# Attention outputs with tokens on the partitions, the sums as a 17th column, and one transpose for the pieces of the maxima

## The chip, the cores and the metric

The kernel runs on one core of a Trainium2 chip. A core has five engines that work side by side, each through its own queue and in its queue's order: TensorE (PE; its weight loads are shown apart as PEld), VectorE (DVE), ScalarE (ACT), GpSimd (POOL) and SyncE (SP), which here only issues DMAs. Matrix products are written to PSUM, everything else lies in SBUF; both have 128 partitions. The metric is the device time of one execution in microseconds.

## The reference

A stack of four decoder layers over x of 16 batches, 128 tokens and 256 features, with a context of the same shape. Every attention has 16 heads of 16 features. Layer 0 attends over the features of one token, layer 1 twice with values rounded to 8 bits. The change is about the four plain attentions, two in layer 2 and two in layer 3:

```python
logits = jnp.einsum('bhqd,bhkd->bhqk', qh, kh) / jnp.sqrt(jnp.float32(depth))
if mask is not None:
    logits = logits + mask * -1000000000.0
attn = jax.nn.softmax(logits, axis=-1)
out = jnp.einsum('bhqk,bhkd->bhqd', attn, vh)
out = out.transpose(0, 2, 1, 3).reshape(Bq, Sq, D)
return out @ wo + bo
```

The first attention of layer 2 has one mask for all batches, the second a mask of keys by batch; of layer 3, the first has none and the second a mask of queries and keys under which a row may be empty. Each is followed by a residual sum, a normalization and, after the second of a layer, a feed-forward block.

## The kernel before

The 16 batches form 8 groups of two (GB = 2, NT = 256 tokens). A group's work is recorded as a list of steps, each with the engines that can do it, a price in microseconds for each, and the blocks that it reads and writes; `Plan.order` then lays out the steps of all groups once, before anything is issued, by those prices, by buffer space and by LEADS, a table of offsets by group and stage. Every engine gets its instructions in that fixed order, so the steps of several groups are interleaved, and a price that is off changes the order and not the work. Four PSUM buffers "pw" of 2 KB a partition and one "ps" of 8 KB serve all groups; "mq" are four small buffers for the pieces named below; everything else lies in one arena in units of 512 B a partition.

TensorE takes fp32 operands here. A matmul uses the whole 128x128 array, or 32 rows of it (four row strips side by side, in the scores), or 32 columns (four column strips, in the products with the values).

A plain attention (`plain_attention`) makes qT and keys with features first: qT is [128 features, 2, 256 tokens], and kz keeps for each pair of heads two copies of the keys, each with the other head's rows zero, so that a strip of 32 rows holds a pair and one of its heads is picked by the copy. The values vz have tokens first; in the attentions over the context, keys and values are made early (`kept_context`), stored to DRAM and loaded again. Then, for each batch j (`batch`):

1. First scores (L833): queries by keys, for all 16 heads, into "ps". VectorE takes the negated maximum of every query and head (L1236; with the common mask in two halves at L1246 and L1251).
2. The 16 maxima of a query are split into three bf16 pieces whose sum is the fp32 number (`split`, L1261 to L1264, POOL or VectorE), written into "mq" as 4 x 128 columns, where head f of strip s has its three pieces at columns 32 s to 32 s + 2 of its own 128. Four bf16 transposes (L1271) turn them and ACT or DVE copies them out as mt (L1275).
3. Second scores, keys by queries: masks where there are any, then the matrix `three`, which adds up three rows of each strip, times mt, 512 columns wide and four strips side by side (L844), then kz by qT on top (L833), all into "ps" again. So the maxima are subtracted inside the matmul, and ACT's exp (L1302, or L1299 after a mask) gives eT with keys on the partitions.
4. Products (`products`, L879): the step `both` multiplies eT by the values and by `ones2`. The values, 32 columns with one of a pair of heads each and zeros for the other, are the stationary operand, 128 columns of eT move, four column strips side by side: 16 matmuls give the outputs with features first and 16 more the sums, already spread over the 16 features of each head.
5. VectorE takes the reciprocal of the sums, 128x256 (L1314), and multiplies (L1315) into oT, which is features first, as the output projection (`tokens_first`, L688) wants it.

The groups' other matmuls are `features_first` (L675), `tokens_first` (L688) and `transposed` (L647, four fp32 transposes of 128x128 and a copy by ACT or DVE at L654).

Of the kernel before, what the change touches and what calls it, by code (L numbers as in the profile page):

```python
# [66 lines left out]
SLOTS = {"sm": (64, 46), "row": (128, 12), "pw": (2048, 4), "ps": (8192, 1), "mq": (1024, 4)}  # L67
# [8 lines left out]
    [83, 27, 167, 130, 306, 193, 74, 226, 213, -45, 163, -53, 159, -84, 116, -64, 214, 400, 286, 283],  # L76
    [-69, -856, -114, -260, -60, 57, -165, -14, -2, -22, -386, -90, 144, -71, -260, -59, -586, -159, -213, -106],
    [49, -47, -11, 314, -162, 407, 51, 168, -361, -27, -172, 141, -4, -107, 36, 5, -54, 235, 78, 92],
    [-16, -228, 250, -173, -19, 106, 36, 203, -176, 14, 164, 2, 299, -144, 10, 309, -45, 154, 150, -1],
    [210, 166, 422, 222, 201, 790, 324, 499, 569, 334, 435, 116, 502, 205, 259, 760, 536, 716, 652, 178],  # L80
    [330, 158, 210, 147, 392, 517, 262, 488, 490, 57, 292, 77, 380, 208, 348, 38, 542, 447, 523, 1141],
    [267, 148, 130, 158, 333, 376, 220, 605, 204, -29, 43, 216, 340, 164, 196, 435, 324, 999, 754, 951],
    [288, 156, 593, 320, 407, 313, 255, 389, 233, 323, -30, 86, 440, 164, 213, 583, 372, 760, 452, 550],
# [344 lines left out]
def decoder_stack_kernel(ctx: ExitStack, tc: tile.TileContext, a: dict, out: bass.AP):  # L428
# [20 lines left out]

    ones2 = const.tile([P, 2, 32], F32, tag="ones2", name="ones2")  # L450
    G.memset(ones2, 0.0)
    for i in range(2):
        G.memset(ones2[:, i, DH * i : DH * i + DH], 1.0)
# [42 lines left out]
    three = const.tile([P, P], BF16, tag="three", name="three")  # L496
    mod = const.tile([P, 32], F32, tag="mod", name="mod")
# [10 lines left out]
    kept = {n: [[drams.tile([P, 4 * NT], F32, tag=f"{n}{g}{i}", name=f"{n}{g}{i}") for i in range(2)] for g in range(NG)] for n in ("mha2", "ca")}  # L508
# [17 lines left out]
    def prepare():  # L526
# [22 lines left out]
        def masks():  # L549

            G.tensor_scalar(later[:, 0:1], mod[:, 0:1], -1.0, 1.0, ALU.mult, ALU.add)
            G.tensor_tensor(later[:, 1:2], later[:, 0:1], mod[:, 1:2], ALU.subtract)
            G.tensor_tensor(three, mod[:, 0:1].to_broadcast([P, P]), mod[:, 1:2].to_broadcast([P, P]), ALU.add)
            G.tensor_tensor(three, three, mod[:, 2:3].to_broadcast([P, P]), ALU.add)

            G.tensor_scalar(m1, m1, -1.0e9, 1.0, ALU.mult, ALU.mult)

        step([("POOL", 2.5, masks)], reads=[raw, dl_token], writes=[mask_token], least=110.0)


# [306 lines left out]
    def products(eTs, vz, j, po, ones=False):  # L867

        def issue():
            for c in range(2):
                for i in range(2):
                    for s in range(4):
                        if ones:
                            lhsT = ones2[:, i, :]
                        else:
                            lhsT = vz.ap()[:, j, 4 * c + s, 2 * i : 2 * i + 2, :].rearrange("p a d -> p (a d)")
                        T.matmul(  # L879
                            po.ap()[32 * s : 32 * s + 32, 2 * ones + c, :], lhsT=lhsT,  # L880
                            rhs=eTs[c].ap()[:, 2 * s + i, :], start=(i == 0), stop=(i == 1),
                        )

        return issue

# [261 lines left out]
    def keys_and_values(kvT, wk, wv, biases, kz, vz):  # L1147
        pk, pv = psum(), psum()
        features_first(weight(wk), kvT, pk, reads=[bias_token], holds=[kz])
        for c in range(2):  # L1150

            def act(c=c):
                for par in range(2):
                    A.activation(
                        kz.ap()[:, c, par, :], pk.ap()[:, c, :], AF.Identity,
                        bias=biases[:, 2 + 2 * par + c : 3 + 2 * par + c], scale=parity[:, par : par + 1],
                    )

            def dve(c=c):
                for par in range(2):  # L1160
                    V.tensor_scalar(
                        kz.ap()[:, c, par, :], pk.ap()[:, c, :], parity[:, par : par + 1],
                        biases[:, 2 + 2 * par + c : 3 + 2 * par + c], ALU.mult, ALU.add,
                    )

            step([("ACT", 0.95, act), ("DVE", 1.06, dve)], reads=[pk], writes=[(kz, c)])
        tokens_first(weight(wv), kvT, pv, holds=[vz])

        def put(eng):
            for j in range(GB):  # L1170
                dst, src = place(vz, j, pv.ap()[:, j, :], None)
                eng(dst, src)

        step([("ACT", 0.8, lambda: put(A.copy)), ("DVE", 0.84, lambda: put(V.tensor_copy))], reads=[pv], writes=[(vz, "v")])

    def kept_context(g, cT):

        there = {}
        for n, layer, at, att in (("mha2", 2, 4, 1), ("ca", 3, 0, 2)):
            plan.enter(after=[*cT.writer.values()], w=RING - 1, kz=1, vz=1)  # L1180
            plan.stage -= 1
            for s in plan.steps[-1:]:
                s.stage = CONTEXT
            plan.special = CONTEXT
            kz, vz = block("m", [P, 2, 2, NT], role="kz"), values(F32)
            wk, wv = (a[w] for w in SQUARE[layer][at + 1 : at + 3])
            keys_and_values(cT, wk, wv, bias_qk[ATT[att]], kz, vz)
            there[n] = []
            for t, d, shape in ((kz, kept[n][g][0], "p c i k -> p (c i k)"), (vz, kept[n][g][1], "p j n q d -> p (j n q d)")):
                token = plan.token()  # L1190
                there[n].append((d, token))
                step([("SP", 2.0, lambda t=t, d=d, shape=shape: nc.sync.dma_start(out=d[:, :], in_=t.ap().rearrange(shape)))], reads=[t], writes=[token])
            plan.special = None
        return there


    def plain_attention(x, qxT, kvT, ws, biases, mask=None, masked=None, cost=0.9, masked_T=None, key_mask=None, held=(), may_be_empty=False, there=None):
# [5 lines left out]
        vz = values(F32) if there is None else block("m", [P, GB, 8, 4, DH], role="vz")  # L1203
# [9 lines left out]
        else:  # L1213
            for t, (d, token) in zip((kz, vz), there):
                step(
                    [("SP", 2.0, lambda t=t, d=d: nc.sync.dma_start(
                        out=t.ap().rearrange("p c i k -> p (c i k)" if len(t.shape) == 4 else "p j n q d -> p (j n q d)"), in_=d[:, :]))],
                    reads=[token], writes=[t] if t is kz else [(t, "v"), (t, "zero")],
# [3 lines left out]
            after=[*qT.writer.values(), *kz.writer.values()], w=1, oT=1, eT=SPREAD, r=1, mt=1, **({"e": 1} if mask is not None else {})  # L1222
        )
        wo = weight(wo)
        oT = block("m", [P, 2, NT], role="oT")

        def batch(j):
# [4 lines left out]
            m, rest, mq = small(16), small(16), block("mq", [P, 4, P], BF16)  # L1232
# [25 lines left out]
            def split(eng, m=m, rest=rest, mq=mq):  # L1258
                piece = lambda n: mq.ap().rearrange("p f (s r) -> p s f r", r=32)[:, :, :, n]
# [7 lines left out]
            pt, mt = block("pw", [P, 4, S], BF16), block("m", [P, 4, S], BF16, role="mt")  # L1267

            def turn(pt=pt, mq=mq):
                for f in range(4):  # L1270
                    T.transpose(pt.ap()[:, f, :], mq.ap()[:, f, :], ident_b)  # L1271

            step([("PE", 0.25, turn)], reads=[mq], writes=[pt], holds=[mt])
            step(
                [("ACT", 0.6, lambda pt=pt, mt=mt: A.copy(mt.ap(), pt.ap())), ("DVE", 0.62, lambda pt=pt, mt=mt: V.tensor_copy(mt.ap(), pt.ap()))],  # L1275
                reads=[pt], writes=[mt],
            )


            def below(ps, mt=mt):  # L1280
                if masked_T is not None:
                    laid(ps, *masked_T)
                laid(ps, lambda s: three[strip(s), :], lambda s: mt.ap()[strip(s)], start=masked_T is None)

            eTs = [block("m", [P, 8, S], role="eT") for _ in range(2)]
            pT, issue = scores(below, lambda r, c, i: kz.ap()[r, c, i, tok], lambda r, c: qT.ap()[r, c, tok], False)
            step(
                [("PE", 1.1 if masked_T is None else 2.1, issue, "rows")],
# [17 lines left out]
            po = block("pw", [P, 4, S])  # L1306
            r = block("m", [P, 2, S], role="r")

            def both(eTs=eTs, po=po, j=j):
                products(eTs, vz, j, po)()  # L1310
                products(eTs, vz, j, po, ones=True)()

            step([("PE", 1.76, both, "cols")], reads=[*eTs, (vz, "v"), (vz, "zero")], writes=[po], holds=[r])
            step([("DVE", 1.75, lambda po=po, r=r: V.reciprocal(r.ap(), po.ap()[:, 2:4, :]))], reads=[po], writes=[r])  # L1314
            step([("DVE", 0.42, lambda po=po, r=r, tok=tok: V.tensor_tensor(oT.ap()[:, :, tok], po.ap()[:, 0:2, :], r.ap(), ALU.mult))], reads=[po, r], writes=[(oT, j)])  # L1315

        for j in range(GB):
            batch(j)
        ps = psum()
# [150 lines left out]
```

## Time and profile before

| | |
|---|---|
| time, median of 3 runs | 1461.99 us (1459.98 to 1463.36) |
| the profiled execution | 1458.82 us, its span 1456.7 us |
| PE busy | 1398.3 us, 96% of the span |
| DVE, ACT, POOL busy | 1010.9, 849.7, 633.3 us |
| mean granted TensorE clock | 0.993 |
| products of plain attention, PE (L879, fp32) | 4096 matmul records in 64 steps |
| reciprocal of the sums, DVE (L1314) | 64 of 1752 ns |
| product with the reciprocal, DVE (L1315) | 64 of 421 ns |
| transposes of the pieces, PE (L1271) | 256 records in 64 steps |
| copies of them, ACT (L1275) | 64 of 582 ns |

Records of matmuls overlap, because they are pipelined: the time that a step takes from PE is read from the start of its first matmul to the start of the next step's. An fp32 matmul leaves two records, a bf16 one and a transpose leave one. The granted clock is the share of full speed that the chip let TensorE run at. In a line of a timeline the columns are the start, the time to the end of the last, engine, line, operation, output and input, shapes and the number of records.

### The profile page before, as it was taken

To read this page: it belongs to the slowest core of one execution; us is meant where nothing else is said; L and a number is where in the kernel's file an instruction comes from. 1 tells how busy PE (TensorE), PEld (TensorE's weight loads), DVE (VectorE), ACT (ScalarE), POOL (GpSimd) and SP (SyncE) were. 2 spreads that over 40 slices of the span, in tenths; PEclk is the share of its full clock that TensorE was granted. 3 is DMA by queue.
4 is the path that set the end of the run, shared out by engine and by line. 5 is a ranking of instruction groups with operands and counts; after the bars stand their busy time and mean duration, and the time that the engine had idled before them with its cause. 6 is when DMAs were issued, how large, how long until landed. Compare 5 with 4: busy or idle time off the path is not lost. (4 is left out here: it accounts for less than half of the span.)

```text
span 1456.7 us, 35756 instructions
## 1 busy us (share of the span) xinstructions
PE 1398.3 (96%) x14771; PEld 1141.3 (78%) x14771; DVE 1010.9 (69%) x1555; ACT 849.7 (58%) x1490; POOL 633.3 (43%) x1415
## 2 busy tenths in 40 slices
PE   8899998999899999899999999999999999999998
PEld 6677887878678888687878777777878888787777
DVE  1665788898988779767764976779478766556431
ACT  4565676766776656565554665657556454445552
POOL 2232857455777446524432542545634234243210
PEclk9999998999999999999999999999999999999999
DMA  6566513412432122112211532211210111100000
GB/s 207 138 171 192 188 48 102 117 34 67 125 90 95 44 67 70 56 52 66 84 38 45 160 101 97 85 55 56 73 45 2 42 38 66 31 31 2 2 9 23
DMA packets 138386, 109.67 MB, mean 75 GB/s; under 512 B 72288, under 2 KB 127472, under 8 KB 138096
## 3 DMA queue, kind: packets, MB, share of 16 engines
q1 hardware_dynamic: 138224, 107.40, 24.5%
q8 instruction: 116, 1.90, 0.5%
q14 instruction: 46, 0.38, 0.1%
HBM read 80.11 MB, written 27.26 MB: 74 GB/s over the span
## 5 line engine op out<-in xcount | busy, mean ns | idle before, releaser
L688 PE MATMUL pw<-arena 128*128 128x256 f32 x2048 | 484.2, 387 | 7.3 <-ACT arena L654 3.1
L675 PE MATMUL pw<-arena 128*128 128x256 f32 x2048 | 480.9, 385 | 7.8 <-ACT arena L663 2.5
L688 PEld LDWEIGHTS pw<-arena 128*128 128x128 f32 x2048 | 383.0, 192 | 68.8 <-issue 9.3
L675 PEld LDWEIGHTS pw<-arena 128*128 128x128 f32 x2048 | 379.2, 191 | 71.0 <-issue 10.0
L1133 POOL TENSOR_SCALAR arena<-arena,sm 128x128 f32<-128x128 f32 x512 | 195.9, 403 | 107.7 <-DVE sm L1127 73.4
L1314 DVE RECIPROCAL arena<-pw 128x256 f32<-128x256 f32 x64 | 112.1, 1752 | 104.0 <-PE pw L879 86.8
L734 POOL TENSOR_TENSOR arena<-arena,rows 128x512 f32<-128x512 f32 x107 | 137.7, 1289 | 89.7 <-ACT arena L721 74.0
L833 PE MATMUL ps<-arena 32*128 32x128 f32 (+2 forms) x3328 | 153.0, 309 | 2.8 <-DVE arena L1112 1.1
L1236 DVE TENSOR_REDUCE sm<-ps 128x16 f32<-128x2048 f32 x48 | 109.6, 2283 | 36.3 <-PE ps L833 33.8
L833 PEld LDWEIGHTS ps<-arena 32*128 32x128 f32 x3072 | 116.1, 186 | 20.4 <-issue 12.0
L696 DVE TENSOR_TENSOR arena<-pw,arena 128x512 f32<-128x512 f32 x88 | 60.3, 685 | 101.2 <-PE pw L688 99.7
L801 ACT ACTIVATE arena<-pw,cols_sb 128x256 f32<-128x256 f32 x184 | 78.0, 472 | 68.3 <-PE pw L675 65.5
L1261 POOL CAST mq<-sm 128x16 bf16<-128x16 f32 x58 | 15.8, 273 | 234.2 <-DVE sm L1236 114.6
L710 POOL TENSOR_SCALAR sm<-sm 128x2 f32<-128x2 f32 x88 | 20.6, 234 | 215.0 <-DVE sm L705 200.1
L721 ACT ACTIVATE arena<-arena,sm,sm 128x256 f32<-128x256 f32 x149 | 83.2, 597 | 49.3 <-POOL sm L714 48.7
L663 ACT ACTIVATE arena<-pw,cols_sb 128x256 f32<-128x256 f32 x140 | 72.7, 563 | 50.5 <-PE pw L647 47.0
L1275 ACT COPY arena<-pw 128x512 bf16<-128x512 bf16 x64 | 37.3, 582 | 84.5 <-PE pw L1271 77.6
L879 PE MATMUL pw<-arena 128*32 128x128 f32 (+1 forms) x2560 | 82.9, 265 | 3.4 <-ACT arena L910 3.0
L1099 DVE TENSOR_REDUCE sm<-ps 128x8 f32<-128x1024 f32 x64 | 77.6, 1213 | 9.8 <-PE ps L833 9.5
L1302 ACT ACTIVATE arena<-ps 128x1024 f32<-128x1024 f32 x64 | 64.1, 1025 | 33.1 <-PE ps L833 30.3
L647 PE MATMUL pw<-ident,arena 128*128 128x128 f32 x416 | 66.8, 286 | 15.1 <-DMA arena<-in_x_dram 5.1
L910 ACT COPY arena<-pw 128x1024 bf16<-128x1024 bf16 x56 | 56.3, 1011 | 41.9 <-PE pw L905 37.2
(142 smaller groups left out, 1993.8 us busy)
## 6 DMA issues: line engine op xcount, KB each, us to landing
arena<-in_L_xattn_ff_w_dram SPq DMA_DIRECT2D x38, 256.0 KB, 3.0
mha<-arena SPq DMA_DIRECT2D x16, 512.0 KB, 4.5
ca<-arena SPq DMA_DIRECT2D x16, 512.0 KB, 3.9
arena<-mha SPq DMA_DIRECT2D x16, 512.0 KB, 4.4
arena<-ca SPq DMA_DIRECT2D x16, 512.0 KB, 4.5
dqkv<-arena SPq DMA_DIRECT2D x8, 768.0 KB, 4.0
arena<-dqkv SPq DMA_DIRECT2D x16, 384.0 KB, 4.3
arena<-in_L_xattn_W_dram SPq DMA_DIRECT2D x24, 256.0 KB, 2.8
```

The source lines that it names most:

```text
L663: ("ACT", 0.54, lambda c=c: A.activation(dst.ap()[:, c, :], ps.ap()[:, c, :], AF.Identity, bias=biases(c), scale=scales(c))),
L675: T.matmul(ps.ap()[:, m, :], lhsT=w.ap()[:, k, m * P : (m + 1) * P], rhs=t.ap()[:, k, :], start=(k == 0), stop=(k == 1),)
L688: T.matmul(ps.ap()[:, j, :], lhsT=lhs(k, j) if lhs else t.ap()[:, k, j * S : (j + 1) * S], rhs=w.ap()[:, k, :], start=start and j + k == 0 ...
L721: ("ACT", 0.6, lambda j=j: A.activation(xh.ap()[:, j, :], x.ap()[:, j, :], AF.Identity, bias=nb.ap()[:, j : j + 1], scale=rstd.ap()[:, j : ...
L734: ("POOL", 1.33, lambda: G.tensor_tensor(dst.ap(), src.ap(), row(name), op)),
L801: "ACT", 0.47, lambda ps=ps, h=h, m=m, bias=bias: A.activation(h.ap()[:, m, :], ps.ap()[:, m, :], func, bias=bias),
L833: T.matmul(ps.ap()[:, s, c] if i is None else ps.ap()[:, s, c, i], lhsT=left(r, c) if i is None else left(r, c, i), rhs=right(r, c), start ...
L879: T.matmul(po.ap()[32 * s : 32 * s + 32, 2 * ones + c, :], lhsT=lhsT, rhs=eTs[c].ap()[:, 2 * s + i, :], start=(i == 0), stop=(i == 1),)
L1099: step([("DVE", 1.22, lambda: V.tensor_reduce(paired(m.ap()), ps.ap()[:, :, c], AX.X, ALU.max, negate=True))], reads=[ps], writes=[m])
L1133: G.tensor_scalar(e.ap()[:, q, :], e.ap()[:, q, :], r.ap()[:, q : q + 1], MAGIC, ALU.mult, ALU.add)
L1236: V.tensor_reduce(m.ap(), ps.ap().rearrange("p s c i k -> p (s c i) k"), AX.X, ALU.max, negate=True)
L1314: step([("DVE", 1.75, lambda po=po, r=r: V.reciprocal(r.ap(), po.ap()[:, 2:4, :]))], reads=[po], writes=[r])
```

## The change

The change concerns step 2 to 5 of every plain attention.

- Values are stored as [tokens, batch, head, 17]: 16 features and a column of ones (`values_with_one`). The kept values shrink from 1024 to 544 numbers a partition. The zeros between the heads and `ones2` go.
- Products: for each head one whole-array matmul, with eT (keys by queries, 128x128) stationary and the head's 17 columns moving. The result po has queries on the partitions: [128, 16 heads, 17], the 17th being the sum.
- VectorE takes the reciprocal of the 16 sums of a query and multiplies 128x256 outputs by it, in one step, into `on`, tokens first. After both batches `transposed` turns `on` into oT with four fp32 transposes and a copy.
- The pieces of the maxima of all 16 heads are packed in 128 columns, strip s having 12 at 32 s. One transpose turns them. In the second scores, `three_of[:, f]` (four matrices, made once on POOL) adds up the three rows of head f of each strip: 16 matmuls of 128 columns, in four rounds of four strips, between the ones of the keys, in the place of 4 of 512 columns.
- The prices of steps are changed where the step is; that of the products stays 1.76. LEADS is another table.

```diff
-SLOTS = {..., "mq": (1024, 4)}
+SLOTS = {..., "mq": (256, 4)}
...
+            for f in range(4):
+                t = three_of[:, f, :]
+                G.tensor_tensor(t, mod[:, 3 * f : 3 * f + 1].to_broadcast([P, P]), mod[:, 3 * f + 1 : 3 * f + 2].to_broadcast([P, P]), ALU.add)
+                G.tensor_tensor(t, t, mod[:, 3 * f + 2 : 3 * f + 3].to_broadcast([P, P]), ALU.add)
...
+    def values_with_one(made):
+        vz = block("m", [P, GB, H, DH + 1], role="vz")
+        if made:
+            step([("POOL", 0.3, lambda: G.memset(vz.ap()[:, :, :, DH : DH + 1], 1.0))], writes=[(vz, "one")])
+        return vz
...
-            pt, mt = block("pw", [P, 4, S], BF16), block("m", [P, 4, S], BF16, role="mt")
-                for f in range(4):
-                    T.transpose(pt.ap()[:, f, :], mq.ap()[:, f, :], ident_b)
+            pt, mt = block("pw", [P, S], BF16), block("m", [P, S], BF16, role="mt")
+            step([("PE", 0.1, lambda pt=pt, mq=mq: T.transpose(pt.ap(), mq.ap(), ident_b))], reads=[mq], writes=[pt], holds=[mt])
...
-                laid(ps, lambda s: three[strip(s), :], lambda s: mt.ap()[strip(s)], start=masked_T is None)
+                for f in range(4):
+                    c, i = divmod(f, 2)
+                    for part in (0, 1) if i else (1, 0):
+                        for s in range(4):
+                            r = strip(s)
+                            T.matmul(
+                                pT.ap()[:, s, c, i], lhsT=kz.ap()[r, c, i, tok] if part else three_of[r, f, :],
+                                rhs=qT.ap()[r, c, tok] if part else mt.ap()[r],
+                                start=..., stop=...,
+                            )
...
-            po = block("pw", [P, 4, S])
-            r = block("m", [P, 2, S], role="r")
+            po, r = block("pw", [P, H, DH + 1]), small(16)
             def both(eTs=eTs, po=po, j=j):
-                products(eTs, vz, j, po)()
-                products(eTs, vz, j, po, ones=True)()
+                for n in range(H):
+                    T.matmul(po.ap()[:, n, :], lhsT=eTs[n // 8].ap()[:, n % 8, :], rhs=vz.ap()[:, j, n, :], start=True, stop=True)
-            step([("PE", 1.76, both, "cols")], ...)
-            step([("DVE", 1.75, lambda po=po, r=r: V.reciprocal(r.ap(), po.ap()[:, 2:4, :]))], reads=[po], writes=[r])
-            step([("DVE", 0.42, ... V.tensor_tensor(oT.ap()[:, :, tok], po.ap()[:, 0:2, :], r.ap(), ALU.mult))], ...)
+            step([("PE", 1.76, both)], reads=[*eTs, vz], writes=[po], holds=[on])
+            def shares(po=po, r=r, j=j):
+                V.reciprocal(r.ap(), po.ap()[:, :, DH])
+                V.tensor_tensor(
+                    on.ap()[:, j, :].rearrange("p (h d) -> p h d", d=DH), po.ap()[:, :, 0:DH], r.ap().unsqueeze(2).to_broadcast([P, H, DH]), ALU.mult,
+                )
+            step([("DVE", 0.65, shares)], reads=[po], writes=[r, (on, j)])
         for j in range(GB):
             batch(j)
+        transposed(on, lambda t: t, copied, oT)
         ps = psum()
         tokens_first(wo, oT, ps)
```

## The prediction

> **What bounds the kernel now.** I read the busy shares of the page first. TensorE's queue is busy 96% of the span and VectorE 69%; in the chain of waits nearly every late step is PE work at L675 and L688 with no wait ahead of it.
>
> ```profile
> PE 1398.3 (96%) x14771; PEld 1141.3 (78%) x14771; DVE 1010.9 (69%) x1555; ACT 849.7 (58%) x1490; POOL 633.3 (43%) x1415
> ...
> L1314 DVE RECIPROCAL arena<-pw 128x256 f32<-128x256 f32 x64 | 112.1, 1752 | 104.0 <-PE pw L879 86.8 <-ACT arena L1302 14.6 <-issue 1.3
> ```
>
> So PE's time is counted at full price and VectorE's at next to nothing: the reciprocal that shrinks stood idle 104 us waiting, mostly for PE. PE's records overlap, so I take a step's price from start to start in the timeline of PE late in the run, where eight groups are interleaved and PE hardly waits.
>
> ```profile
> 1404.65 0.38 PE L688 MATMUL pw<-arena 128*128 128x256 f32 x1
> 1404.96 1.08 PE L879 MATMUL pw<-arena 128*32 128x128 f32 x32
> 1405.85 1.06 PE L879 MATMUL pw<-arena,ones 128*32 128x128 f32 x32
> 1406.84 1.04 PE L844 MATMUL ps<-m3T,ident_b 128*128 128x512 bf16 x4
> 1407.81 0.39 PE L844 MATMUL ps<-arena,three 32*128 32x512 bf16 x4
> 1408.04 1.06 PE L833 MATMUL ps<-arena 32*128 32x128 f32 x32
> 1409.03 0.40 PE L1271 MATMUL pw<-ident_b,mq 128*128 128x128 bf16 x4
> 1409.26 0.43 PE L688 MATMUL pw<-arena 128*128 128x256 f32 x1
> ```
>
> See three things. An fp32 matmul leaves two records (16 matmuls, x32), each with its own weight load; I call one a pass. Values and ones together take 1.88 us (1404.96 to 1406.84). And the pass before them holds PE for 0.31 us where such passes else follow each other every 0.216 us (next fence: 56 in 12.10 us): changing from the whole array to strips costs 0.095 us, and about 0.11 us of the 1.88 is the same on the way back, so the products themselves are 1.77 us.
>
> ```profile
> 1440.72 12.10 PE pw L688 x56
> ```
>
> What matters for the new form is how long a whole-array fp32 weight load takes when no long matmul hides it. First the groups by form (mean ns of one after the comma), then the loads and the matmul of one step that starts after a wait:
>
> ```profile
> L688 PEld LDWEIGHTS pw<-arena 128*128 128x128 f32 x2048 | 383.0, 192 | 68.8 <-issue 9.3 <-ACT arena L654 3.9 <-ACT arena L1105 2.1
> ...
> L879 PEld LDWEIGHTS pw<-arena,ones 128*32 128x32 f32 x2048 | 57.2, 110 | 0.0
> ```
> ```profile
> 79.24 0.48 PE L688 MATMUL pw<-arena 128*128 128x256 f32 x1 [0.28 <-DVE arena L696]
> ```
> ```profile
> 79.24 0.30 PEld L688 LDWEIGHTS pw<-arena 128*128 128x128 f32 x2 [0.49 <-DVE arena L696]
> ```
>
> A 128-column load is recorded 82 ns longer than a 32-column one: 0.85 ns a column, 109 ns for 128. At 79.24 the first matmul is 0.48 us where its group's mean is 0.387, and two loads span 0.30 us where one is 0.19: the second starts 0.108 us after the first. In the middle of a run 216 ns of streaming hide those 108 ns.
>
> Last, the granted clock, which, once the start is over, falls to a half four times before the last matmul, in stretches of 3.41 us or a multiple. The first line of each pair is the stretch before, the second the half-clock one; the last pair shows a thin stretch that was not followed by a drop.
>
> ```profile
> 50.46:53.88 3.42, 0.55 (x5) 1.00 0.90 264
> 53.88:57.29 3.41, 3.41 (x36) 0.50 0.21 55
> ...
> 589.77:593.18 3.41, 1.76 (x14) 1.00 0.62 231
> 593.18:596.60 3.42, 3.42 (x20) 0.50 0.00 0
> 842.36:845.77 3.41, 1.55 (x11) 1.00 0.00 0
> 845.77:849.18 3.41, 3.41 (x124) 1.00 0.14 14
> ```
>
> The stretch at 589.77 holds 4 fp32 transposes, 2 mask matmuls of 512 columns and 8 bf16 transposes, which stream 4 x 107 + 2 x 213 + 8 x 53 ns = 1.28 us, 0.38 of it; the one at 842.36 streams 1.39 us, 0.41. So a stretch in which the array streams under about 0.39 of the time cost the next one half its clock, though PE was far from idle in it.
>
> **The change, part by part.**
>
> *Products.* 64 times (8 groups, 4 attentions, 2 batches) 32 strip matmuls become 16 whole-array ones with 17 columns moving: 32 passes. A pass streams 216 x 17/256 = 14 ns and waits for its own load, 108 ns: 3.46 us for 1.77, +1.69 each, +108 us in all. Lower bound: passes as short as a strip's load, 0.85 x 32 = 27 ns, 0.87 us, -58 us; upper: loads not overlapped at all, their whole record of 192 ns, 6.1 us, +277 us. I take 108 ns: it is the same operation, only with a short stream behind it. The step's price in the kernel's plan stays 1.76 us, so the order written from it has PE early; nothing waits longer for that but PE's own successors.
>
> [...]
>
> *Shape changes.* The two orders of instructions have 495 changes of array shape before and 410 after: 85 x 0.095 = -8 us.
>
> *Transposes of the outputs.* 32 attentions gain four fp32 transposes; four such at L647 go from start to start in 0.50 us:
>
> ```profile
> 1416.83 0.66 PE L647 MATMUL pw<-ident,arena 128*128 128x128 f32 x4
> 1417.33 1.89 PE L688 MATMUL pw<-arena 128*128 128x256 f32 x8
> ```
>
> +16 us. They wait for VectorE's shares of the second batch, and output projection and residual wait for them; behind them in PE's queue stand other groups' matmuls. The wait is new, but po is now normalized in one short step instead of 1752 + 421 ns, so it starts 1.5 us sooner.
>
> *Maxima.* Four bf16 transposes (1409.03 to 1409.26, 0.23 us) become one: -0.17 x 64 = -11 us.
>
> *Second scores.* 1407.81 to 1409.03 is 1.22 us for the sums of pieces and the keys. After: 8 rounds of four strips for the keys at 0.11 (the 0.99 us of L833 over 8, less the 0.1 on the way out), 4 bf16 rounds of 128 columns at 0.056, and twice a key load that a short bf16 round covers only half, 0.05: 1.22. Zero, with -0.2 (bf16 rounds wholly hidden) to +0.3 us (every change of type exposes a load) as ends: -13 to +19 us.
>
> *Costed at nothing.* VectorE loses about 1.5 us x 64 = 96 us (reciprocal and division, 2.17, for 16 reciprocals and a 128x256 product, about 0.65), all beside PE. ScalarE's copy of the pieces halves (64 x 0.3 saved), 32 copies of 0.59 us come; at 58% it has room. POOL gets eight more mask operations of 0.4 us (the row of L553), 3.2 us once, some 200 us ahead of the first scores at 315, and smaller memsets (L861 takes 0.52 now). On SP the kept values go from 512 to 272 KB a transfer. Were that cover gone, the mask operations would cost 3 us and the copies 19.
>
> *Stalls.* PE's waits that the groups show sum to some 50 us, 32 of them after 320 us where attention runs (380, 400 and 357 us that hold 367, 389 and 348 us of busy PE). A PE that is slower by 100 us while VectorE has 96 us less to do waits less: -12 us, between 0 and -30.
>
> Sum: 108 - 8 + 16 - 11 + 0 - 12 = +93. The profiled execution took 1458.8 us (span 1456.7), the median shown is 3.2 above it: 1552 profiled, 1555 as a median, if the clock stays.
>
> *The clock.* It need not stay. In a product step the array streams 14 of 108 ns, 0.13. A step is 3.46 us, a stretch 3.41. With neighbours that stream 0.93 (the rest being stalls and shape changes, 50 + 47 us of 1457), a stretch falls under 0.39 when products fill more than (0.93 - 0.39) / (0.93 - 0.13) = 0.68 of it. With stretches that start anywhere, that happens in 2 x 0.32 = 0.65 of the steps: 42 stretches at half clock, each losing up to 1.7 us, less where the stretch holds the rest of a product step; at 1.55, +65 us, 1620. If loads count as activity too, it is 0 and the time 1555. Rows say "streaming": the 14 matmuls at 589.77 had their loads as well, and PE's queue was busy 1.76 of 3.41 us.
>
> [...]
>
> **Rivals.**
> - *The clock holds* (1555): for it, nothing before runs load-bound, so no row shows whether loads count. Chance 0.33.
> - *Loads overlap better than I think* and a pass takes 55 ns, as the plan's price implies (1.76 / 32). Then the step costs what it did, the sum is -8 + 16 - 11 - 12 = -15 and the time about 1447; it ends faster from 62 ns a pass down (64 x 32 passes: 2.05 us of time for each ns). Against it: 108 ns at 79.24. Chance 0.05.
> - *Low stretches chain*: half clock stretches the next product step, which keeps the clock down. Twice as many half stretches would give 1685. Chance 0.06; the stretch after is mostly full work, which let the clock back at once at 57.29 and 596.60.
>
> **How the numbers follow.** Likeliest, 0.56: products at 108 ns and about 42 half-clock stretches, 1620, its own range 1590 to 1650. The range given reaches down to the case of the steady clock with its second scores at the low end (1555 - 15) and up to 1655. A difference under 0.2% is about what a measurement of this kernel can't tell from no change; only the second rival ends faster, and between it and 1540 there is little: faster 0.04, same 0.01, slower 0.95.
>
> **What would show it.** Load records of the products at 190 ns starting every 108 ns and steps of about 3.4 us; PEclk digits under 9 through the slices from 320 us on, and a mean granted clock near 0.95 (42 x 3.41 us at half). Wrong if product passes start faster than 60 ns, or if the clock stays at 0.99.

## The result and the profile after

The changed kernel takes 1682.8 us, median of 4 runs; the kernel before, on the same chip, 1462.7. The ratio is 1.150 (95% interval 1.148 to 1.152); it leaves out one of the four runs, which took 1707.9 us at a granted clock of 0.910, where the others had 0.924 to 0.926. The profiled execution took 1681.8 us, its span 1680.0, against 1458.8 and 1456.7.

First the busy shares of the page of after, and the row of the granted clock over 40 slices of the span.

```profile
PE 1614.3 (96%) x13427; PEld 1359.3 (81%) x13427; DVE 921.5 (55%) x1564; ACT 835.4 (50%) x1460; POOL 615.8 (37%) x1422
...
PEclk9999979799989999799998989899989888999989
```

TensorE has 1344 matmul records fewer and is busy 216 us longer, at the same 96% of the span; VectorE has 89 us less to do. The clock falls under 9 in 12 of 40 slices, in the kernel before in one; its mean went from 0.993 to 0.924. Then the groups by form (busy us, mean ns of one, idle time ahead and what ended it).

```profile
L1319 PEld LDWEIGHTS pw<-arena 128*128 128x128 f32 x2048 | 252.5, 202 | 6.6 <-issue 2.4 <-DVE arena L790 0.3 <-ACT arena L802 0.3
L1319 PE MATMUL pw<-arena 128*128 128x17 f32 x2048 | 250.7, 270 | 0.0
...
L1324 DVE RECIPROCAL sm<-pw 128x16 f32<-128x16 f32 x64 | 16.5, 257 | 255.7 <-PE pw L1319 255.7
```

The reciprocal became seven times shorter, 257 ns for 1752, and the time that VectorE stands idle in front of it grew from 104 to 256 us, all of it waiting for the products. Two product steps from PE's timeline, the first at full clock, the second at half:

```profile
834.03 0.81 PE L689 MATMUL pw<-arena 128*128 128x256 f32 x3
834.68 3.64 PE L1319 MATMUL pw<-arena 128*128 128x17 f32 x32
838.17 0.59 PE L845 MATMUL ps<-m3T,ident_b 128*128 128x512 bf16 x2
```
```profile
677.72 1.06 PE L676 MATMUL pw<-arena 128*128 128x256 f32 x2
678.57 6.85 PE L1319 MATMUL pw<-arena 128*128 128x17 f32 x32
685.35 0.61 PE L845 MATMUL ps<-arena,three 32*128 32x512 bf16 x4
```

From 834.68 to 838.17 is 3.49 us for 32 passes, one every 109 ns; from 678.57 to 685.35 it is 6.78, about 212 ns a pass. The step was 1.77 us before.

**Where the 223 us of span came from.** For every kernel below I added up the starts of PE's matmul records by step, each from its first record to the next step's. The work at full clock is, for each kind of step, the lower quartile of its steps outside the half-clock stretches, times their number. What a step took over that inside a half-clock stretch is loss to the clock, up to half of its time; what is left is waits. By this rule:

| us of span | work at full clock | loss to the clock | waits |
|---|---|---|---|
| before, 1457 | 1329 | 10 | 96 |
| after, 1680 | 1453 | 121 | 83 |
| difference | +124 | +111 | -13 |

(The span's beginning and end, some 22 us, lie outside.) The clock's column is firm to some 4 us. Work and waits trade some 10 to 20 us when the same traces are grouped into steps another way (by line, output and number of records, before comes to 1341, 10 and 84, after to 1458, 124 and 75), so smaller differences between these two columns say little. About half of the loss is work, nearly all of it in the products, and half is the clock. The granted clock itself says the same: (1 - 0.924) x 1680 = 128 us against (1 - 0.993) x 1457 = 10. The list of waits shows nothing of either: PE's largest single line in it is 5.7 us.

**How the clock falls.** Five stretches of 3.41 us of after (length, PE's busy time and records, granted clock, share of the DMA engines, GB/s):

```profile
672.96:676.37 3.41, 3.41 (x29) 1.00 0.25 76
676.37:679.79 3.42, 3.42 (x13) 0.50 0.00 1
679.79:683.20 3.41, 3.41 (x18) 0.50 0.00 0
683.20:686.61 3.41, 3.41 (x24) 0.50 0.00 0
686.61:690.03 3.42, 3.42 (x31) 0.50 0.00 0
```

And three others, the first of which lies all but wholly inside one product step:

```profile
744.55:747.96 3.41, 3.41 (x33) 1.00 0.00 0
747.96:751.37 3.41, 3.41 (x19) 0.51 0.00 0
751.37:754.79 3.42, 3.42 (x17) 0.99 0.00 0
```

By its records PE is busy for all 3.41 us of each. But the share of the time in which the array streams at least one matmul's columns (an estimate: 0.833 ns a column for an fp32 pass at full clock, half of what passes of 256 columns take at half clock, where they follow each other every 427 ns at L676, and every 216 at full; half of that in bf16, of which 512 columns take 426 and 216 ns at L845) is 0.26 at 672.96, 0.71 at 676.37, 0.13 and 0.45 in the two after it, and 0.94 at 686.61, behind which the clock is full again. The stretch inside the product step streams 0.13, the next is half-clocked, streams 0.83, and the clock is let back.

### The profile page after: what moved, and what is told of

Same layout as the page of the kernel before. It is cut to its first block, busy times and chain, and to the rows that moved or that the text cites. A ratio compares the mean times of both kernels' runs of the same rounds, so it can differ in the third digit from the quotient of the medians.

```text
span 1680.0 us, 32904 instructions
## 1 busy us (share of the span) xinstructions
PE 1614.3 (96%) x13427; PEld 1359.3 (81%) x13427; DVE 921.5 (55%) x1564; ACT 835.4 (50%) x1460; POOL 615.8 (37%) x1422
## 4 chain that ended last, share of the span: by engine, by line
PE 88%; DVE 5%; ACT 2%; POOL 2%; issue 1%; DMA 1%; SPq 0%; POOLq 0%; DVEq 0%; ACTq 0%
PE pw L676 26%; PE pw L689 26%; PE pw L1319 14%; PE ps L1290 6%; PE ps L834 5%; PE pw L648 4%; PE ps L845 2%; PE pw L910 2%; POOL arena L1138 1%; DVE sm L1104 1%; DVE arena L1117 1%; PE pw L1024 1%; PE pw L991 1%; ACT arena L967 1%; DVE arena L966 1%
## 5 line engine op out<-in xcount | busy, mean ns | idle before, releaser
L676 PE MATMUL pw<-arena 128*128 128x256 f32 x2048 | 502.1, 398 | 5.5 <-ACT arena L915 1.8
L689 PE MATMUL pw<-arena 128*128 128x256 f32 x2048 | 495.8, 395 | 6.9 <-DVE arena L1003 3.6
L676 PEld LDWEIGHTS pw<-arena 128*128 128x128 f32 x2048 | 395.7, 199 | 70.0 <-issue 4.1
L689 PEld LDWEIGHTS pw<-arena 128*128 128x128 f32 x2048 | 394.2, 198 | 70.1 <-issue 5.8
L1319 PEld LDWEIGHTS pw<-arena 128*128 128x128 f32 x2048 | 252.5, 202 | 6.6 <-issue 2.4
L1319 PE MATMUL pw<-arena 128*128 128x17 f32 x2048 | 250.7, 270 | 0.0
L1324 DVE RECIPROCAL sm<-pw 128x16 f32<-128x16 f32 x64 | 16.5, 257 | 255.7 <-PE pw L1319 255.7
L1290 PE MATMUL ps<-arena 32*128 32x128 f32 x2048 | 110.7, 327 | 7.2 <-ACT arena L1311 5.7
L655 ACT COPY arena<-pw 128x512 f32<-128x512 f32 x75 | 43.5, 585 | 143.9 <-PE pw L648 139.1
L802 ACT ACTIVATE arena<-pw,cols_sb 128x256 f32<-128x256 f32 x190 | 80.6, 472 | 63.2 <-PE pw L676 60.1
L1290 PEld LDWEIGHTS ps<-arena 32*128 32x128 f32 x2048 | 85.4, 210 | 26.4 <-issue 12.9
L648 PE MATMUL pw<-ident,arena 128*128 128x128 f32 x544 | 94.2, 308 | 8.9 <-POOL bias_qk L579 5.1
L1311 ACT ACTIVATE arena<-ps 128x1024 f32<-128x1024 f32 x64 | 64.1, 1024 | 74.6 <-PE ps L1290 64.0
L834 PE MATMUL ps<-arena 32*128 32x256 f32 (+1 forms) x1280 | 93.9, 404 | 5.8 <-DVE arena L1117 5.5
```

Source lines behind the costliest of these rows:

```text
L648: T.transpose(p[:, c, j * S : (j + 1) * S], s[:, j, c * P : (c + 1) * P], ident)
L676: T.matmul(ps.ap()[:, m, :], lhsT=w.ap()[:, k, m * P : (m + 1) * P], rhs=t.ap()[:, k, :], start=(k == 0), stop=(k == 1),)
L689: T.matmul(ps.ap()[:, j, :], lhsT=lhs(k, j) if lhs else t.ap()[:, k, j * S : (j + 1) * S], rhs=w.ap()[:, k, :], start=start and j + k == 0 ...
L802: "ACT", 0.47, lambda ps=ps, h=h, m=m, bias=bias: A.activation(h.ap()[:, m, :], ps.ap()[:, m, :], func, bias=bias),
L834: T.matmul(ps.ap()[:, s, c] if i is None else ps.ap()[:, s, c, i], lhsT=left(r, c) if i is None else left(r, c, i), rhs=right(r, c), start ...
L1290: T.matmul(pT.ap()[:, s, c, i], lhsT=kz.ap()[r, c, i, tok] if part else three_of[r, f, :], rhs=qT.ap()[r, c, tok] if part else mt.ap()[r], ...
```

## The experiments

The theory from the traces: (1) a stretch in which the array streams less than about 0.39 of the time, which is between the 0.38 at 589.77 and the 0.41 at 842.36 of before, costs the next one half its clock, and loads don't count; (2) a pass of the products costs its 128-column load; (3) the rest is the order of the work. The rivals were that the half clock comes from something else of the changed kernel (its order, its waits), and that the new order or its waits carry the loss. All ratios are to the kernel before on the same chip.

| kernel | us, median | ratio (95%) | work | clock | waits |
|---|---|---|---|---|---|
| after | 1682.8 | 1.150 (1.148 to 1.152) | 1453 | 121 | 83 |
| 1 wide stream | 1599.9 | 1.096 (1.094 to 1.097) | 1453 | 34 | 88 |
| 2 four strips | 1469.8 | 1.008 (1.005 to 1.011) | 1311 | 33 | 99 |
| 3 old table | 1747.8 | 1.194 (1.187 to 1.201) | 1449 | 131 | 122 |
| 4 maxima alone | 1523.8 | 1.044 (1.042 to 1.046) | 1333 | 35 | 130 |
| 5 two strips | 1503.3 | 1.028 (1.026 to 1.031) | 1367 | 38 | 75 |
| 6 strips, sums first | 1465.0 | 1.002 (1.001 to 1.004) | 1308 | 36 | 95 |
| 7 searched table, a | 1479.4 | 1.012 (1.010 to 1.014) | 1299 | 32 | 128 |
| 8 searched table, b | 1472.4 | 1.008 (1.006 to 1.011) | 1296 | 26 | 129 |
| 9 maxima, order kept | 1463.4 | 1.003 (1.002 to 1.004) | 1329 | 10 | 98 |
| 10 before, new table | 1620.1 | 1.111 (1.109 to 1.113) | 1328 | 68 | 205 |
| 11 as 9, sums first | 1457.0 | 0.9965 (0.9951 to 0.9979) | 1323 | 19 | 96 |

The last three columns are us of the profiled execution, by the rule above.

**1. Is it the thin stream?** The changed kernel with 68 columns moving instead of 17 and everything else, the order included, as it was. The head's own 17 columns come first and the 51 behind them are overwritten by the next heads' matmuls, so this multiplies more than it needs.

```diff
-T.matmul(po.ap()[:, n, :], lhsT=eTs[n // 8].ap()[:, n % 8, :], rhs=vz.ap()[:, j, n, :], ...)
+m = min(n + 4, H)
+T.matmul(po.ap()[:, n:m, :]..., lhsT=eTs[n // 8].ap()[:, n % 8, :], rhs=vz.ap()[:, j, n:m, :]..., ...)
```

> The changed kernel with 68 columns moving in a product instead of 17: each matmul also multiplies the next three heads' values, into places that the following matmuls overwrite, so the output stays. Passes, loads and order are the same; only the stream of a pass grows from 14 to 57 ns, hidden under its load of 111. Theory (the clock follows the share of time in which the array streams): product steps stay at 3.5 us at full clock, half-clock time falls from 256 us to under 100, the time to 1560-1610 us. Rival (the clock falls because PE waits in the new order, or because loads are not work however long the stream): half-clock time and time stay, 1665-1695 us.

Measured: 1599.9 us, 83 less than after (80 by the ratios). The same step and the stretches of 3.41 us from its start, and the clock's row of its page:

```profile
726.73 3.64 PE L1320 MATMUL pw<-arena 128*128 128x68 f32 x32
730.22 0.63 PE L648 MATMUL pw<-ident,arena 128*128 128x128 f32 x4
```
```profile
726.72:730.13 3.41, 3.41 (x33) 1.00 0.00 0
730.13:733.54 3.41, 3.41 (x26) 1.00 0.00 0
```
```profile
PEclk9999989799999999999999999989999999999999
```

The step takes 3.49 us as before, so the work is the same 1453 us, with up to four times the columns; but no product step is followed by a half-clock stretch any more, where 38 were, and the loss to the clock is 34 us for 121. This settles two things: a pass of these products is bound by its load (3.49 us a step with 17 columns and with 68), and the loss of 80 to 87 us comes from the thin stream of the products. What stays, 22 half-clock stretches, 15 of them before 440 us where no product has run in this order, is not theirs.

**2 and 5. Is it the width of the load?** The stationary eT is cut into strips of 32 or 64 columns, so that four or two loads and matmuls of a head can run side by side. The same products, the same order.

```diff
+for s in range(4):
+    T.matmul(po.ap()[strip(s), n, :], lhsT=eTs[n // 8].ap()[:, n % 8, strip(s)], rhs=vz.ap()[:, j, n, :], ...)
```

In number 5, `range(2)` and `half = slice(64 * s, 64 * s + 64)` in the place of `strip(s)`.

> The changed kernel with each product cut into four column strips of 32 queries: eT's 32 columns are stationary, the same 17 columns move, 64 matmuls and 128 passes a step, prices and order kept. Theory (a whole-array load of 128 columns is the price, and strips load side by side): a round of four passes lasts about 28 ns, a step 0.9-1.2 us instead of 3.5, the array streams half the time in it so the clock stays; 160 us of work and about 100 us of half clock go: 1410-1450 us. Rival 1 (loads of strips follow one another, 128 x 27 ns): a step of 3.5 us, 1640-1700 us. Rival 2 (the new order is what costs): above 1550 us.

> The changed kernel with each product cut into two column strips of 64 queries, order kept: 32 matmuls and 64 passes a step, each loading 64 columns. Theory (a load costs by its columns and strips load side by side): a round of two passes about 57 ns, a step 1.8-1.95 us between the 1.2 of four strips and the 3.5 of the whole array; the array streams 14 of 57 ns, but a step fills only half a stretch of the clock, so the products cause no drop: 1480-1520 us. Rival (loads follow one another): a step of 3.5 us and the drops stay, 1640-1700 us.

Measured: 1469.8 and 1503.3 us. A step of each, four strips and then two, from PE's timelines:

```profile
1041.71 1.27 PE L1320 MATMUL pw<-arena 128*32 128x17 f32 x128
1042.91 0.33 PE L648 MATMUL pw<-ident,arena 128*128 128x128 f32 x1
```
```profile
788.62 2.05 PE L1321 MATMUL pw<-arena 128*64 128x17 f32 x64
790.60 0.60 PE L845 MATMUL ps<-m3T,ident_b 128*128 128x512 bf16 x2
```

Steps of 1.20, 1.98 and 3.49 us for loads of 32, 64 and 128 columns: a round takes 38, 62 and 109 ns, which in the first two steps includes the changes of shape, as an estimate some 0.2 us a step from the 0.095 and 0.11 us of before. The step's price by columns held (two strips 0.03 us above the range), and for two strips the time with it. For four strips the step was as expected, but the time was 20 us above my range. The work fell by 142 us, the clock's loss by 88, and the waits rose by 16; I had forgotten that the new order has half-clock stretches of its own (20 here, 1 of them behind a product), and that the products are now 4 times as many instructions. Its groups have waits called "issue" there, time for which the profile shows no cause; that the instructions reach PE late is my reading of it:

```profile
L1320 PE MATMUL pw<-arena 128*32 128x17 f32 x8192 | 85.7, 187 | 4.9 <-issue 4.8
...
L1320 PEld LDWEIGHTS pw<-arena 128*32 128x32 f32 x8192 | 78.9, 110 | 24.0 <-issue 20.0 <-ACT arena L722 2.0 <-DVE arena L790 0.3
```

**6. The second scores.** As number 2, with the sums of pieces of all four heads ahead of the keys instead of between them, so that the type changes once.

```diff
-for f in range(4):
-    for part in (0, 1) if i else (1, 0):
+for part in (0, 1):
+    for f in range(4):
```

> The kernel of four column strips with the second scores in another order: the 16 matmuls that add up the pieces come first, then all keys, instead of alternating. Same instructions, prices and order of steps. Theory (in the changed order the first load of keys and two more stand bare, each some 0.1 us; with the sums first one short one does): the step falls from 1.43 to 1.22-1.30 us, 64 times 0.13-0.2 us less: 1455-1463 us. Rival (changes between bf16 and fp32 cost nothing, the step is bound elsewhere): 1466-1474 us, unchanged.

Measured: 1465.0 us, just above what I expected; the step went from 1.433 to 1.279 us, which was the price expected. So the alternation costs 0.15 us a step, 10 us in all; by the ratios 8 us of that, within 4 either way, reached the time.

**3 and 10. The table of offsets.** Number 3 is the changed kernel with LEADS of the kernel before; number 10 the kernel before with LEADS of the changed one and nothing else.

```diff
-LEADS = [[178, 127, 182, ...], ...]
+LEADS = [[83, 27, 167, ...], ...]
```

> The changed kernel with the table LEADS of the kernel before, so another order of steps. Theory (products and clock): full-clock work unchanged, half-clock time 200-300 us, the time within 30 us of 1680. Rival (the new table's order costs): most of the 220 us go, under 1560 us.

> The kernel before with the table LEADS of the changed kernel, nothing else. Theory (a table fits the prices that it was searched for): waits and half-clock time grow as in e4 and e3 or more, full-clock work within 15 us of the kernel before: 1500-1650 us. Rival (the new table is as good for the old steps): within 20 us of 1460.

Measured: 1747.8 us and 1620.1. The profiled execution of number 3, to which its last three columns belong, took 1726.8, the shortest of its four runs by 19 us. The page of number 10:

```profile
PE 1443.4 (89%) x14771; PEld 1170.9 (72%) x14771; DVE 1009.4 (62%) x1567; ACT 831.8 (51%) x1456; POOL 640.2 (40%) x1411
...
PEclk9999999799978999889999999999999999999978
```

The work is the old kernel's (1328 us for 1329), waits grow by 109 us and the clock's loss by 58; that the second comes of the first is my reading. Each kernel loses with the other's table: 65 us the changed one, where I expected less than 30, and 162 us the old one, by its ratio. So each table suits the kernel that it came with, and another order can cost as much as the products did. The old table would not have spared the changed kernel its loss, and experiment 6 comes within 0.2% of the kernel before in the new order; a table searched for whole-array products at their true price was not tried.

**4, 9 and 11. The maxima alone.** The kernel before with the packed pieces, one transpose and the sums of pieces in four rounds; products as before. Number 4 takes the changed kernel's prices for those steps; number 9 the old prices and the old size of mt, so that the order is that of the kernel before; number 11 is number 9 with the sums first, as in number 6.

```diff
 # 4
-step([("PE", 0.25, turn)], reads=[mq], writes=[pt], holds=[mt])
+step([("PE", 0.1, lambda pt=pt, mq=mq: T.transpose(pt.ap(), mq.ap(), ident_b))], ...)
 # 9: the same work under ("PE", 0.25), ("ACT", 0.6), ("PE", 1.1), ("POOL", 2.5), mt of [P, 4, S]
```

> The kernel before with the pieces packed into one transpose and the second scores as changed, products and LEADS as before. Theory: 11 us less for transposes, 14 us more for second scores (1.43 us a step for 1.215): 1455-1475 us, clock at 0.98 or more. Rival (the packed pieces take part in the clock's fall or in the waits): above 1480 us.

> The kernel before with the pieces packed into one transpose and the second scores as changed, as in e4, but with the prices and block sizes of the steps left as they were before, so that all steps stand in the order of the kernel before. Theory (e4's 60 us came from another order, made by other prices under a table of offsets searched for the old ones): transposes -11, second scores +14 us of work, the rest as before: 1458-1472 us, clock at 0.985 or more. Rival (the packed pieces or the alternating matmuls themselves make PE wait): above 1500 us.

> The kernel of e9 (products and order of the kernel before, one transpose for the packed pieces) with the sums of the pieces ahead of all keys in the second scores, as in e6. Theory (the step falls from 1.43 to 1.28 us where every step keeps its place): 64 times 0.155 us less than e9's 1463, 1450-1456 us, under the kernel before by 0.3 to 0.6%. Rival (in a fixed order the time saved in one step is waited away at the next): 1458-1464 us.

Measured: 1523.8, 1463.4 and 1457.0 us. The longest waits of PE in number 4 (what PE waited for, us in all, times, longest):

```profile
PE ps L850 <- DVE sm L1242: 12.7, 7, 2.4
PE pw L681 <- ACT arena L669: 9.1, 13, 1.4
```

Number 4 missed by 49 us, and number 9 says why: the same instructions in the old order cost 4 us instead of 64, by the ratios. Prices that were changed by 0.05 to 0.4 us, and by 2.5 for the masks, together with the smaller mt, reshuffled the whole order, to 34 us more of waits and 25 us more of clock loss than in the kernel before. Which of them did it, and how such waits come about, was not followed further.

The clock's row of number 9 is that of the kernel before, digit for digit:

```profile
PEclk9999998999999999999999999999999999999999
```

Number 11, 1 us above the range expected, beats both kernels, the one before by 0.35% (0.21 to 0.49). By the ratios it is 9 us under number 9, where 64 x 0.155 = 10 us were expected: in a fixed order the step's saving reached the time. Its profiled execution, 1460.3 us at a clock of 0.987, is the slowest of its 12 runs, so the profile doesn't show the gain; the two shortest runs, 1451.5 and 1452.2 us, had 0.993 and 0.995.

**7 and 8. A table for the true prices.** As number 6, with the products priced at 1.1 us and the second scores at 1.22, and two LEADS tables searched on the plan's own model.

```diff
-step([("PE", 1.76, both)], reads=[*eTs, vz], writes=[po], holds=[on])
+step([("PE", 1.1, both, "cols")], reads=[*eTs, vz], writes=[po], holds=[on])
+LEADS = [...]
```

> Four column strips and sums first, with the products priced at 1.1 us plus a change of shape and the second scores at 1.22 instead of 1.76 and 1.15, and a table LEADS searched for those prices: another order of the same instructions. Theory (full-clock work of TensorE is 20 us under the kernel before; the rest was half clock and waits of an order made for other prices): half-clock time under 60 us and waits no more than before: 1435-1455 us, under the kernel before. Rival (the longer chain with the outputs' transposes, or fetching of 2.5 times as many instructions in the products, keeps PE waiting in any order): 1458-1480 us.

> The same kernel as the run before with another table from the same kind of search, 2 us longer by the prices of the plan. Theory: within 12 us of that run. Rival (an order's waits and clock on the chip are not what its prices say): more than 20 us off.

Measured: 1479.4 us, expected at 1435 to 1455, and 1472.4, within 12 us of that as expected, but 7 us shorter where the plan's prices made it 2 us longer. The work is 30 us less than before, and waits take 32 us more, the clock's loss 22 and 16. PE's largest wait in number 7:

```profile
PE pw L1321 <- issue: 16.4, 17, 2.1
```

The only such wait of PE in the kernel before:

```profile
PE pw L986 <- issue: 2.9, 1, 2.9
```

The profile names no other engine. In the strips' products PE stands so 17 times, where the changed kernel and number 5, with two strips, have no such wait at all. That its instructions come late there is what this suggests; no run tests it. The plan's model knows neither these waits nor the clock, and a better order by it was no better on the chip.

## Why the prediction was wrong in size

It said 1620, range 1540 to 1655, and slower with 0.95. The direction and most terms held; the time lies 28 us above the range.

| term | predicted, us | measured, us |
|---|---|---|
| products, 64 steps | +108 | +110 (3.49 us for 1.77) |
| shape changes | -8 | -11 |
| transposes of the outputs | +16 | +14 |
| maxima's transposes | -11 | -11 |
| second scores | 0 (-13 to +19) | +14 |
| stalls | -12 | -6 |
| clock | +65 | +111 |
| sum | +158, 1617 to 1620 | +221, against 223 of span |

(The shape changes are read from the steps at L675 and L688 next to the products. The stalls are the -13 of waits and some 7 us in which PE stood at L612 of after; the rule counts these as work, because both steps of L612 touch half-clock stretches.)

**Right.** The pass costs its load, and 108 ns from the two loads at 79.24 was within 4 ns of what 2048 passes then took (109 by the step, 112 from start to start). Four column strips paid here for a stationary operand of 128 columns: 1.20 us a step in the second experiment, against 1.77 in the kernel before, where eT moves and the values are stationary, but which also multiplies by zeros and takes the sums in 16 matmuls of their own. What I had set at nothing for VectorE, ScalarE and POOL stayed off the path: the waits didn't grow (83 us for 96). And in these traces the clock followed the streamed share; load records didn't keep it up: at 744.55 PE's records fill all of the 3.41 us, the array streams 0.13 of it, and the next stretch has a clock of 0.51.

**Wrong, 46 us: the clock's term.** I counted 42 product steps that drop the clock; 38 did. There were 75 half-clock stretches, and each lost 1.61 us (121 / 75), near the 1.55 I took. The step that failed is the count of stretches, twice. "The stretch after is mostly full work, which let the clock back at once" made each drop one stretch; it was 1.34 on average (51 / 38). And the half clock that the new order has apart from the products was put at nothing, without a reason; it came to 24 stretches, and is the larger part of the miss:
- Chains. The 38 drops by products gave 51 stretches. No half-clock stretch that streamed under 0.72 of its time was followed by a full one, and the rest of a product step can keep a stretch under that: at 676.37 it streams 0.71, at 679.79 0.13, at 683.20 0.45, each followed by half clock. I had a rival of this kind, at 1685 with a chance of 0.06. That the time came out near its total is luck: its mechanism gave 13 stretches more, about 21 us, and not the 42 that it supposed.
- The order's own half stretches. 24 have no product behind them, against 6 half-clock stretches of any cause before; 16 of the 24 lie before 440 us, ahead of the first product step of this order at 442 us. Experiments 1, 2 and 6, with other products in the same order, have most of them too (22, 19 and 23, of which 14 or 15 before 440 us); experiment 9, in the old order, has 6. These drops are of another kind: ahead of each of the nine chains that make up the 24, PE's records fill only 0.00 to 1.68 of the 3.41 us (none at 297.50, 1.10 at 212.16, 1.37 at 1079.20), so PE stood waiting in the new order, where the products drop the clock with PE busy throughout. I had counted shape changes in the changed order, and not looked in it for thin stretches.

Together: 51 and 24 stretches at 1.61 are 82 and 39 us, less 10 of before: 111. Of the 46 us, 17 are the products' 82 for 65, and 29 the order's own 39 less 10.

**Wrong, 14 us: the second scores.** I took them unchanged at 1.22 us; they take 1.43. In PE's timeline of after:

```profile
1120.35 0.50 PE L1290 MATMUL ps<-arena 32*128 32x128 f32 x8
1120.68 0.29 PE L1290 MATMUL ps<-arena,three_of 32*128 32x128 bf16 x8
1120.79 0.68 PE L1290 MATMUL ps<-arena 32*128 32x128 f32 x16
1121.29 0.29 PE L1290 MATMUL ps<-arena,three_of 32*128 32x128 bf16 x8
1121.40 0.46 PE L1290 MATMUL ps<-arena 32*128 32x128 f32 x8
1121.79 0.28 PE L1319 MATMUL pw<-arena 128*128 128x17 f32 x1
```

The first eight key records take 0.33 us where two rounds at 0.11 would be 0.22: as I read it, the first load has no sums of 512 columns ahead of it any more to hide it. And the last eight take 0.39, the way out of the row strips included, which I had left out of the new sum and had in the old one. The sixth experiment, which puts the sums first, gets 0.15 of the 0.22 us back.

**Wrong, 6 us: the stalls**, which shrank by half of what I gave them; that is less than the grouping of steps can move the waits.

Idle gaps of PE don't explain the drops by products: at 744.55 PE has no gap in 3.41 us of records, and the next stretch runs at half clock; and the first experiment gave 83 us back while the waits went from 83 to 88 us.

## What to carry to other kernels

Price a matmul by the longer of its stream and its weight load, as the passes here went: one every 216 ns with 256 columns moving and 128 stationary, and 109 ns with 17 or 68, where the load is everything. Cutting the stationary operand into four column strips bought most of it back (38 ns a round), at the price of four times the instructions. When such thin matmuls fill some 3 us (a product step took 3.49), add up the streamed columns for each 3.41 us, the length of a stretch here, not PE's busy time, and ask of each half-clock stretch whether it holds enough work: here those under 0.72 stayed at half. In a kernel whose order is planned from prices, change one part with the old prices first: with new prices or another table the order alone moved 60 to 160 us here, and hid what the edit did.

## What the runs showed of the hardware

- The granted clock and the share of a stretch in which the array streams, as estimated above from the lengths of passes. Over the 13 traces, in stretches of 3.41 us (the counts near the ends of the middle ranges move by a few with where in its record a stream is taken to lie): at full clock, all 188 with a share under 0.36 were followed by a half-clock one, 12 of 40 between 0.36 and 0.41, and 1 of 5159 above. At half clock, all 153 under 0.72 stayed at half, 11 of 16 between 0.72 and 0.78, none of 195 above. The traces of before and after alone give 48 of 48, 3 of 10 and none of 764, and at half clock 29 of 29, 1 of 2 and none of 50. That the streaming is what counts is inferred from these shares; experiment 1, which changed only the columns, is the direct test: 38 drops behind products became none, and the loss to the clock 34 us for 121.
- Loads of column strips and their matmuls overlap: a round of four loads of 32 columns, each recorded with 110 ns, took 38 ns (experiment 2), one of two loads of 64 columns, recorded with 142, 62 (experiment 5), one load of 128 columns 109 (after). At half clock a pass with 128 columns to load took 212 ns (678.57 of after).
- In front of the products with four times as many matmuls, 4.8, 4.1 and 16.4 us of "issue" waits of PE stand in experiments 2, 6 and 7, and none with twice as many (experiment 5) or as many (after). That PE waits for its own instructions is inferred.
